# A planned graph network stack: picks and messages in fewer engines, and a planner that counts PE's results as late

## The chip, the cores and the metric

The kernel runs on one NeuronCore of a Trainium2 chip. The metric is the device time of one execution in microseconds (us). The engines are named as in the profile: PE (TensorE, matmuls; PEld its weight loads), DVE (VectorE), ACT (ScalarE), POOL (GpSimd) and SP (SyncE, which here only issues DMAs).

## The reference

Four layers of a graph network over 4096 nodes of 128 features, with one adjacency matrix `adj` of 4096x4096, float32, in which about one entry in a thousand is set, more in the first rows and columns. Every layer adds its result to `x`:

```python
# before each layer
h = jnp.maximum(_layernorm(x, axis=-1), 0.0)
# layer 0
x = x + h @ W_self.T + (adj @ h) @ W_neigh.T + b
# layer 1: Chebyshev terms T0 = h, T1 = adj @ h, T2 = 2 * adj @ T1 - T0
x = x + T0 @ w[0] + T1 @ w[1] + T2 @ w[2] + bias
# layer 2: attention
H = h @ weight.T
C = alpha_src[None, :] + alpha_dst[:, None]
Tau = adj.T * jnp.exp(jnp.maximum(0.2 * C, C))
att = Tau / jnp.sum(Tau, axis=1, keepdims=True)
x = x + adj.T * att @ H
# layer 3: messages
messages = gelu(s[:, None, :] + d[None, :, :] + msg_b)        # s, d = h @ msg_w halves
aggregated = jnp.einsum('ijd,ij->id', messages, adj)
f = gelu(concat([h, aggregated]) @ upd_w.T + upd_b) + h
x = x + layernorm(f) * ln_w + ln_b
```

## The kernel before, in words

**Sparse work from a dense matrix.** The nodes are sorted so that full rows come first. The kernel reads `adj` once (`read_adj`, `mark`, `scan`), makes flags of it, and from these, on the chip, three kinds of lists: for stripes of 256 rows and of 256 columns the lists of nodes that they touch (`pairs`), and for every block of 128 rows the list of its entries (`entries`). A list is cut in chunks of 128 places, one for each partition. All through the kernel, rows are fetched by such lists with indirect DMAs that POOL issues, one for each chunk (line 553 for all of them): 68 chunks of row lists, 74 of column lists and 158 of entries.

**Stages.** First the scan, with the first product of layer 0 (`Layer.multiply`, line 1138 for the near blocks, 1155 for the fetched rows). Then the products of the layers 0 to 2, while `entries` makes the entry lists and `values` fetches their values into `e_val`. Then `Attention`, by column stripes (1228 to 1254), with `finish_3` behind each stripe. Then `Messages`, by groups of four blocks: `prepare`, `message` for every four chunks of entries, `finish` for the last norm and the store. Where the buffers allow it, stages overlap; the messages of the first block may start under the attention.

**The picks** (in `entries`, lines 882 to 894). For up to four chunks, PE multiplies a selection matrix `sel` with the tables `A` and `B` into a PSUM bank of the kind `picks`: positions in columns 0 to W, differences of codes in W to 2W. ACT copies the positions to SBUF (`ehit`, 887), and DVE does one scalar_tensor_tensor for each chunk (890), which compares with the place's own number, multiplies with the differences and sums up into `packed`.

**A message** (`message`, 1391). For up to four chunks it needs: a selection `sel` (622, 624), the matrices `r` with the edge values (1400), the fetched rows `m` of `d_tab` (553), then in a PSUM bank of the kind `banks` the sum of `m` (a product with the identity, 1406) and of the block's own rows picked by `sel` (1408), then the gelu by ACT out of the bank (1412), and the product with `r` into the accumulator of the group (1418).

**The last norm** (`finish`, 1425). DVE makes the mean (1445, 1446), ACT the squares (1450) and the root (1453), DVE the reciprocal and mean times reciprocal (1455, 1456), ACT the scaled copies, one for each block (1459), DVE the weights and sums (1463 to 1465), SP the store (1467).

**The order.** Every piece of work is a task, a generator that yields what it wants next: an engine with an estimate of its time, a free buffer of a kind (`Slots`), or an event. `Plan.run` (299) simulates all tasks in the time of these estimates and at each step lets the one go on that can begin first, or, among those within 0.3 us of it on the same engine, the one with the lowest rank. What it picks is emitted there and then, and `in_order` (348) binds every engine to that order. A step that changes its engine begins `HOP` = 0.2 us after the one before at the earliest (315). Where the plan leaves PE idle for more than 0.8 us, `fill` (604) puts products with zeros into a bank or a pick that is free (609), one for each 0.22 us of 80% of the gap. The kinds that matter here: three `banks`, two `picks`, three `accs`; for messages four tiles `m`, two `r` and one lane with `sel` under the attention, and twelve, four and four afterwards, when the free `picks` join the `banks`. The ranks of the gathers: products and attention 0, columns' segments 4, values of entries 6, the first block's messages 7.

Of the kernel before, what the change touches and what calls it, by code (L numbers as in the profile page):

```python
# [19 lines left out]
AF = mybir.ActivationFunctionType  # L20
ALU = mybir.AluOpType
AX = mybir.AxisListType
# [4 lines left out]
D = 128  # L27
P = 128
# [3 lines left out]
GB = BANK // D  # L32
# [222 lines left out]
class Plan:  # L255
# [4 lines left out]


    HOP = 0.2
    LANDING = 4.0
    BYTES = 330e3
    TABLE = 1.3
# [33 lines left out]
    def run(self, until=lambda: False):  # L299
        while self.tasks and not until():  # L300
            able = []
            for task in list(self.tasks):
                while isinstance(task.want, Event) and task.want.time is not None:
                    if task.want.time + self.HOP > task.ready:
                        task.ready, task.engine = max(task.ready, task.want.time), None
                    self._next(task)
                want = task.want
                if want is None or isinstance(want, Event):
                    continue
                if isinstance(want, Slots):  # L310
                    if not want.free:
                        continue
                    begin = max(task.ready, min(want.free)[0])
                else:
                    begin = max(task.ready + self.HOP * (task.engine != want[0]), self.free[want[0]])
                able.append((begin, task.rank, task.serial, task))
            assert able, [(t.generator.__name__, t.want) for t in self.tasks]
            first = min(able)
            want = first[3].want
            if not isinstance(want, Slots):  # L320

                first = min((a[1:] for a in able if a[0] <= first[0] + min(self.PATIENCE, want[1]) and
                             not isinstance(a[3].want, Slots) and a[3].want[0] == want[0]))
                first = next(a for a in able if a[3] is first[2])
            begin, task = first[0], first[3]
            want = task.want
            if isinstance(want, Slots):
                first = min(want.free)
                want.free.remove(first)
                task.ready = begin  # L330
                self._next(task, want.items[first[1]])
                continue
            duration = want[1]
            if want[0] == "PE":
                duration *= self.PE_TIME
                gap = begin - self.free["PE"]
                if self.filler and gap > self.SHORT:
                    self.filler(self.free["PE"], gap * self.FILLED)
            self.finish = begin + duration
            if len(want) > 2 and want[2] != self.table:  # L340
                self.table = want[2]
                self.finish += self.TABLE
            self.free[want[0]] = self.finish
            task.ready, task.engine = self.finish, want[0]
            self._next(task)
# [12 lines left out]
def on_dve(n):  # L358
    return "DVE", 0.16 + 1.05e-3 * n
# [7 lines left out]
def on_act(n, table=None):  # L367
    return ("ACT", 0.22 + 0.83e-3 * n) + ((table,) if table else ())
# [10 lines left out]
def sparse_stack(tc, x, adj, adjT, diag, w_self, w_neigh, b0, w1, b1, w2, att_src, att_dst,  # L379
# [7 lines left out]
    nc = tc.nc  # L387
    plan = Plan()
    EARLY = 7
    with ExitStack() as ctx:  # L390
# [212 lines left out]

        def fill(begin, time):

            idle = min((free, i, slots.items) for slots in (banks, picks) for free, i in slots.free + [(1e9, 0)])
            if idle[0] < begin - 1.0:
                for _ in range(int(time / 0.22)):
                    nc.tensor.matmul(idle[2][idle[1]], nothing[:, :P], nothing, start=True, stop=True)  # L609

        def rows_of(p, n=GB):
            return p[:, :n * D].rearrange("p (k d) -> p k d", d=D)
# [192 lines left out]
        def entries(number, group):  # L805
# [65 lines left out]
            for i, u in enumerate(units):  # L871
                for g in range(-(-u.cap // GB)):
                    n = min(GB, u.cap - g * GB)
                    yield from selection(lane, mids[:, u.number, :], half[:, u.number:u.number + 1], g, n)
                    for q0 in range(0, n, per):
                        m = min(per, n - q0)
                        k = g * GB + q0
                        p = yield picks
                        pv = p[:, :m * (2 * W + 1)].rearrange("p (q w) -> p q w", w=2 * W + 1)
                        yield "PE", m * (0.3 + 1.3e-3 * W)  # L880
                        for q in range(m):
                            sel = lane["sel"][:, q0 + q, :]
                            nc.tensor.matmul(pv[:, q, :], sel, A[:, i, :], start=True, stop=False)  # L883
                            nc.tensor.matmul(pv[:, q, W:2 * W], sel, B[:, i, :], start=False, stop=True)
                        yield on_act(m * W)
                        hit = lane["ehit"][:, :m * W].rearrange("p (q w) -> p q w", w=W)
                        nc.scalar.copy(hit, pv[:, :, :W])  # L887
                        yield "DVE", m * (0.2 + 1.05e-3 * W) + 0.15
                        for q in range(m):
                            nc.vector.scalar_tensor_tensor(  # L890
                                hit[:, q, :], hit[:, q, :], pos0[:, k + q:k + q + 1], pv[:, q, W:2 * W],
                                op0=ALU.is_le, op1=ALU.mult, accum_out=packed[:, u.chunk + k + q:u.chunk + k + q + 1])
                        nc.vector.tensor_copy(e_row[:, u.chunk + k:u.chunk + k + m], pv[:, :, 2 * W])
                        plan.release(picks, p)
            lo, hi = units[0].chunk, units[-1].chunk + units[-1].cap
# [420 lines left out]
        class Messages:  # L1316
# [74 lines left out]
            def message(self, g, b, u, c, chunks, m, here):  # L1391
                n = len(chunks)
                yield u_done[u.number]
                lane = yield m_lanes
                yield from selection(lane, mids[:, u.number, :], half[:, u.number:u.number + 1], c, n)
                yield self.s_here[g]
                r = yield r_tiles
                yield "DVE", 0.35 * n
                for q, k in enumerate(chunks):
                    nc.vector.tensor_scalar(r[:, q, :], iota_row[:, :P], e_row[:, k:k + 1], e_val[:, k:k + 1],  # L1400
                                            op0=ALU.is_equal, op1=ALU.mult)
                for q in range(n):
                    yield here[q]
                p = yield banks
                yield "PE", n * 0.84
                nc.tensor.matmul(p[:, :n * D], ident, m[:, :n, :], start=True, stop=False)  # L1406
                for q in range(n):
                    nc.tensor.matmul(p[:, q * D:(q + 1) * D], lane["sel"][:, q, :], self.s_rows[g][:, b % GB, :],  # L1408
                                     start=False, stop=q == n - 1)
                plan.release(m_lanes, lane)  # L1410
                yield on_act(n * D, "gelu")
                nc.scalar.activation(m[:, :n, :], rows_of(p, n), AF.Gelu)
                plan.release(banks, p)
                yield "PE", 0.42 * n
                acc = self.acc[g]
                for q in range(n):
                    self.left[b] -= 1
                    nc.tensor.matmul(acc[:, b % GB * P:(b % GB + 1) * P], m[:, q, :], r[:, q, :], start=False,  # L1418
                                     stop=all(self.left[g * GB + k] == 0 for k in range(GB)))
                plan.release(r_tiles, r)  # L1420
                plan.release(messages, m)
                if all(self.left[g * GB + k] == 0 for k in range(GB)):
                    plan.start(self.finish(g), -2)

            def finish(self, g):
# [27 lines left out]
                nc.scalar.activation(st[:, 1, :GB], st[:, 1, :GB], AF.Sqrt, bias=eps, scale=1.0 / D)  # L1453
                yield "DVE", 0.35
                nc.vector.reciprocal(st[:, 2, :GB], st[:, 1, :GB])
                nc.vector.tensor_mul(st[:, 3, :GB], st[:, 0, :GB], st[:, 2, :GB])
                yield "ACT", 0.45 * GB
                for k in range(GB):
                    nc.scalar.activation(f[:, k, :], f[:, k, :], AF.Identity, scale=st[:, 2, k:k + 1],
                                         bias=st[:, 3, k:k + 1])  # L1460
                plan.release(stats, st)
                yield "DVE", 2.1
                nc.vector.tensor_mul(f, f, by_block(ln_w_sb, GB))
                nc.vector.tensor_add(f, f, by_block(ln_b_sb, GB))
                nc.vector.tensor_add(f, f, xN[:, blocks, :])
# [521 lines left out]
```

## Time and profile before

| | us |
|---|---|
| three runs | 1508.06, 1502.92, 1518.15 |
| median | 1508.06 |
| the profiled execution: its own time | 1500.43 |
| its span, from the first to the last instruction | 1498.6 |

| engine | busy us | share of the span | instructions |
|---|---|---|---|
| PE | 1058.5 | 71% | 5943 |
| DVE | 791.5 | 53% | 2982 |
| ACT | 670.3 | 45% | 1344 |
| POOL | 767.3 | 51% | 832 |

The mean granted PE clock is 0.834 of full speed. 216 us of PE's busy time are the products with zeros of line 609. Busy shares are means over stages with different limits. In a line of the waits stand the waiting engine, tile and line, what ended the wait, the sum in us, the number and the longest; in a line of the timeline start, duration, engine, line, operation, tiles and shapes, and in brackets the idle time of the engine ahead of it with what ended it. "issue" means that the profile shows no reason, "remote" and "another core or an unknown queue" that a semaphore came from where the profile can't tell. A group of instructions in the timeline is merged into one line, with x and the number.

### The profile page before, as it was taken

How to read it: one execution, taken by the hardware profiler on the slowest of the kernel's cores; microseconds unless marked ns; L12 is line 12 of the kernel's file. 1: busy time of each engine (PE TensorE's matmuls, PEld its weight loads, DVE VectorE, ACT ScalarE, POOL GpSimd, SP SyncE). 2: the span in 40 equal slices, each digit the busy share in tenths (PEclk: the TensorE clock that was granted, in tenths of full speed). 3: DMA queues.
4: the chain of work that ended last, by engine and by line, in shares of the span. 5: the costliest groups of instructions: out<-in, count | busy, mean ns of one | idle time of the engine just before them, and what ended most of it. 6: DMA issues, size and time to landing. Idle time of an engine off the chain costs nothing.

```text
span 1498.6 us, 19187 instructions
## 1 busy us (share of the span) xinstructions
PE 1058.5 (71%) x5943; PEld 723.0 (48%) x5943; DVE 791.5 (53%) x2982; ACT 670.3 (45%) x1344; POOL 767.3 (51%) x832
## 2 busy tenths in 40 slices
PE   6786788887477867467774289668777955668880
PEld 3454555554256556355653255334444633556660
DVE  5796666886366566355663156334343612344453
ACT  5983666663121212114452087546564801236462
POOL 4135754544455656635667527726576165654500
PEclk9897898888697888677897599879897986888885
DMA  8999999994366778666542045313333121121200
GB/s 252 352 338 318 335 308 342 341 310 145 92 194 191 205 217 232 171 193 176 156 132 80 22 123 146 108 39 87 107 101 97 41 59 43 47 51 48 67 17 17
DMA packets 175415, 236.03 MB, mean 157 GB/s; under 512 B 22452, under 2 KB 155336, under 8 KB 167112
## 3 DMA queue, kind: packets, MB, share of 16 engines
q1 hardware_dynamic: 148904, 186.45, 37.6%
q0 software_dynamic: 26400, 48.27, 13.1%
q8 instruction: 49, 0.80, 0.2%
q14 instruction: 62, 0.51, 0.1%
HBM read 203.41 MB, written 31.23 MB: 157 GB/s over the span
## 4 chain that ended last, share of the span: by engine, by line
PE 26%; issue 11%; ACT 9%; another core or an unknown queue 8%; DVE 5%; DMA 1%; SPq 0%; ACTq 0%; DVEq 0%
PE acc L1254 4%; PE acc L1252 4%; PE bank L597 3%; PE acc L1138 3%; PE acc L1155 2%; PE acc L1418 2%; PE pick L609 1%; PE bank L1406 1%; PE bank L1408 1%; ACT e L1228 1%; ACT junk L1450 1%; ACT e L1231 1%; ACT junk L568 1%; PE pick L1418 1%
## 5 line engine op out<-in xcount | busy, mean ns | idle before, releaser
L553 POOL DMA_INDIRECT e_val<-in_adj,e_at x158 | 155.5, 984 | 48.0 <-issue 46.5
L553 POOL DMA_INDIRECT g<-h_tab,fetch_row x136 | 135.7, 998 | 73.1 <-issue 34.3
L609 PE MATMUL pick<-nothing 128*128 128x512 f16 x532 | 141.4, 413 | 2.4 <-issue 2.4
L1138 PE MATMUL acc<-big,hA 128*128 128x256 f32 x448 | 124.6, 422 | 16.3 <-DMA big<-in_adjT 7.3
L609 PEld LDWEIGHTS <-nothing 128*128 128x128 f16 x795 | 83.5, 108 | 102.7 <-issue 38.3
L553 POOL DMA_INDIRECT g<-a_tab,fetch_col x74 | 77.7, 1049 | 92.5 <-issue 43.6
L553 POOL DMA_INDIRECT rseg<-in_adjT,seg_row x68 | 71.3, 1048 | 94.3 <-issue 39.7
L1138 PEld LDWEIGHTS acc<-big,hA 128*128 128x128 f32 x448 | 90.6, 213 | 32.8 <-DMA big<-in_adjT 8.8
L553 POOL DMA_INDIRECT cseg<-in_adj,seg_col x74 | 70.8, 957 | 66.2 <-DVE pcum L634 23.5
L553 POOL DMA_INDIRECT g<-u_tab,fetch_row x68 | 64.7, 951 | 63.7 <-PE acc L1155 32.5
L890 DVE SCALAR_TENSOR_TENSOR ehit<-ehit,pos,pick 128x32 f32<-128x32 f32 (+7 forms) x158 | 38.8, 285 | 108.0 <-issue 64.6
L1235 DVE TENSOR_TENSOR tau<-e,big 128x512 f32<-128x512 f32 (+3 forms) x61 | 54.2, 889 | 70.2 <-ACT e L1231 43.7
L887 ACT COPY ehit<-pick 128x192 f32<-128x192 f32 (+7 forms) x74 | 20.4, 286 | 157.8 <-remote 72.5
L553 POOL DMA_INDIRECT tau<-d_tab,e_col x63 | 60.5, 961 | 56.2 <-PE acc L1418 15.1
L553 POOL DMA_INDIRECT m<-d_tab,e_col x70 | 68.0, 972 | 38.0 <-issue 16.5
L768 ACT ACTIVATE mask<-dst 128x2048 fp8e4<-128x2048 f32 x43 | 81.8, 1903 | 12.1 <-DMA dst<-in_adj 9.5
L1155 PE MATMUL acc<-big,g 128*128 128x256 f32 x272 | 80.8, 437 | 2.7 <-DMA big<-r_tab 1.9
L622 ACT ACTIVATE sel_t<-iota_row,mids 128x512 f32<-128x512 f32 (+3 forms) x43 | 27.1, 642 | 118.1 <-DVE mids L617 69.8
L568 ACT ACTIVATE junk<-xN,stat 128x128 f32<-128x128 f32 x128 | 51.4, 401 | 60.7 <-DVE stat L564 23.1
L609 PE MATMUL bank<-nothing 128*128 128x512 f16 x263 | 74.8, 430 | 1.6 <-DVE s L1369 1.2
L883 PE MATMUL pick<-eA,esel 128*128 128x65 f16 (+7 forms) x158 | 27.3, 249 | 61.4 <-DVE esel L624 24.1
L1138 PE MATMUL acc<-big,hB 128*128 128x256 f32 x224 | 64.2, 428 | 0.0
(328 smaller groups left out, 2727.5 us busy)
## 6 DMA issues: line engine op xcount, KB each, us to landing
dst<-in_adj SPq DMA_DIRECT2D x43, 1024.0 KB
big<-in_adjT SPq DMA_DIRECT2D x45, 512.0 KB
raw<-in_adj SPq DMA_DIRECT2D x21, 1024.0 KB
big<-in_adjT SPq DMA_DIRECT2D x66, 256.0 KB
big<-r_tab SPq DMA_DIRECT2D x30, 512.0 KB
c_tab<-cseg SPq DMA_DIRECT2D x74, 128.0 KB
r_tab<-rseg SPq DMA_DIRECT2D x68, 128.0 KB
big<-c_tab SPq DMA_DIRECT2D x15, 512.0 KB
```

The lines of the kernel that those rows point to most:

```text
L553: nc.gpsimd.indirect_dma_start(out=dst, out_offset=None, in_=table[:, :], in_offset=bass.IndirectOffsetOnAxis(ap=index, axis=0))
L568: nc.scalar.activation(junk, src[:, k, :], AF.Square, bias=st[:, 0, k:k + 1], accum_out=st[:, 1, k:k + 1])
L597: nc.tensor.matmul(p[:, k * D:(k + 1) * D], lhs[:, k * P:(k + 1) * P], w, start=i == 0, stop=i == len(terms) - 1)
L609: nc.tensor.matmul(idle[2][idle[1]], nothing[:, :P], nothing, start=True, stop=True)
L768: nc.scalar.activation(mask[:, h * HALF:(h + 1) * HALF], raw_of[b, h], AF.Sigmoid, scale=1e38, accum_out=marks[:, 2 * b + h:2 * b + h + 1] ...
L890: nc.vector.scalar_tensor_tensor(hit[:, q, :], hit[:, q, :], pos0[:, k + q:k + q + 1], pv[:, q, W:2 * W], op0=ALU.is_le, op1=ALU.mult, acc ...
L1138: nc.tensor.matmul(acc, self.near[:, b, :D], as_rows(t)[:, k, :], start=count == 0, stop=count == every - 1)
L1155: nc.tensor.matmul(acc, row[:, :D], r, start=count == 0, stop=count == every - 1)
L1235: nc.vector.tensor_mul(tau[:, :n, :], e[:, :n, :], a[:, :n, :])
L1252: nc.tensor.matmul(acc[0:1, CS:2 * CS], parts[k][:, D + 1:], tau[:, k, :], start=False, stop=False)
L1254: nc.tensor.matmul(acc[:, :CS], parts[k][:, :D], e[:, k, :], start=False, stop=self.count[s.index] == every - 1)
L1418: nc.tensor.matmul(acc[:, b % GB * P:(b % GB + 1) * P], m[:, q, :], r[:, q, :], start=False, stop=all(self.left[g * GB + k] == 0 for k in ...
```

## The change

- The planner gets a second constant, `LATE` = 1.5: a step on another engine that follows a step on PE in the same task begins 1.5 us behind it, not 0.2, in the plan. All other handovers keep 0.2.
- `fill` compares free buffers by time and number alone.
- The picks: ACT's copy goes. DVE compares out of PSUM for all chunks of the group at once, multiplies with the differences out of PSUM, and sums up with a tensor_reduce.
- The messages: PE takes a bank and does the selection's product alone, without waiting for the fetched rows, and gives the lane back; then the rows are waited for, DVE adds the bank to them in SBUF and gives the bank back, and ACT does the gelu in SBUF.
- The last norm: mean and reciprocal are applied by DVE, one tensor_scalar for each block; the small product of both goes.

```diff
     HOP = 0.2
+    LATE = 1.5
...
-                    begin = max(task.ready + self.HOP * (task.engine != want[0]), self.free[want[0]])
+                    hop = self.LATE if task.engine == "PE" else self.HOP
+                    begin = max(task.ready + hop * (task.engine != want[0]), self.free[want[0]])
...
-            idle = min((free, i, slots.items) for slots in (banks, picks) for free, i in slots.free + [(1e9, 0)])
+            idle = min(((free, i, slots.items) for slots in (banks, picks) for free, i in slots.free + [(1e9, 0)]),
+                       key=lambda slot: slot[:2])
...
-                        yield on_act(m * W)
+                        yield "DVE", 0.6 + 3.2e-3 * m * W
                         hit = lane["ehit"][:, :m * W].rearrange("p (q w) -> p q w", w=W)
-                        nc.scalar.copy(hit, pv[:, :, :W])
-                        yield "DVE", m * (0.2 + 1.05e-3 * W) + 0.15
-                        for q in range(m):
-                            nc.vector.scalar_tensor_tensor(
-                                hit[:, q, :], hit[:, q, :], pos0[:, k + q:k + q + 1], pv[:, q, W:2 * W],
-                                op0=ALU.is_le, op1=ALU.mult, accum_out=packed[:, u.chunk + k + q:u.chunk + k + q + 1])
+                        nc.vector.tensor_tensor(hit, pv[:, :, :W], pos0[:, k:k + m, None].to_broadcast([P, m, W]),
+                                                op=ALU.is_le)
+                        nc.vector.tensor_mul(hit, hit, pv[:, :, W:2 * W])
+                        nc.vector.tensor_reduce(packed[:, u.chunk + k:u.chunk + k + m], hit, axis=AX.X, op=ALU.add)
                         nc.vector.tensor_copy(e_row[:, u.chunk + k:u.chunk + k + m], pv[:, :, 2 * W])
...
+                p = yield banks
+                yield "PE", n * 0.42
+                for q in range(n):
+                    nc.tensor.matmul(p[:, q * D:(q + 1) * D], lane["sel"][:, q, :], self.s_rows[g][:, b % GB, :],
+                                     start=True, stop=True)
+                plan.release(m_lanes, lane)
                 for q in range(n):
                     yield here[q]
-                p = yield banks
-                yield "PE", n * 0.84
-                nc.tensor.matmul(p[:, :n * D], ident, m[:, :n, :], start=True, stop=False)
-                for q in range(n):
-                    nc.tensor.matmul(p[:, q * D:(q + 1) * D], lane["sel"][:, q, :], self.s_rows[g][:, b % GB, :],
-                                     start=False, stop=q == n - 1)
-                plan.release(m_lanes, lane)
+                yield on_dve(n * D)
+                nc.vector.tensor_add(m[:, :n, :], m[:, :n, :], rows_of(p, n))
+                plan.release(banks, p)
                 yield on_act(n * D, "gelu")
-                nc.scalar.activation(m[:, :n, :], rows_of(p, n), AF.Gelu)
-                plan.release(banks, p)
+                nc.scalar.activation(m[:, :n, :], m[:, :n, :], AF.Gelu)
...
-                nc.vector.tensor_mul(st[:, 3, :GB], st[:, 0, :GB], st[:, 2, :GB])
-                yield "ACT", 0.45 * GB
                 for k in range(GB):
-                    nc.scalar.activation(f[:, k, :], f[:, k, :], AF.Identity, scale=st[:, 2, k:k + 1],
-                                         bias=st[:, 3, k:k + 1])
+                    nc.vector.tensor_scalar(f[:, k, :], f[:, k, :], st[:, 0, k:k + 1], st[:, 2, k:k + 1], op0=ALU.add,
+                                            op1=ALU.mult)
                 plan.release(stats, st)
-                yield "DVE", 2.1
+                yield "DVE", 3.3
```

## The prediction

> **What bounds the kernel now.** I read the page first (shares, chain), then the waits, the chain stage by stage, and the timeline where the chain shows holes. The page ends its span with a chain in which no engine dominates:
>
> ```profile
> span 1498.6 us, 19187 instructions
> PE 26%; issue 11%; ACT 9%; another core or an unknown queue 8%; DVE 5%; DMA 1%; SPq 0%; ACTq 0%; DVEq 0%
> ```
>
> PE holds 26%, but 19% is "issue" or "another core or an unknown queue": nobody worked. (The chain is followed back only to about 595 us.) The list of waits says who stands idle for reasons that the profile can't name:
>
> ```profile
> ACT ehit L887 <- remote: 72.5, 7, 29.2
> PE bank L597 <- issue: 72.5, 13, 44.3
> DVE ehit L890 <- issue: 64.6, 20, 26.9
> ACT tau L1412 <- remote: 61.4, 3, 35.2
> POOL e_val L553 <- issue: 46.5, 153, 0.3
> ```
>
> This is one core, so "remote" can't be another one. L887 and L1412 are the ScalarE instructions that read a PE result in the picks and in the messages: exactly the two hops that go. The timeline shows what they wait for; columns are start, duration, instruction, idle time before it:
>
> ```profile
> 1211.43 1.05 PE L1408 MATMUL bank<-s,msel 128*128 128x128 f32 x8
> 1216.56 0.60 ACT L1412 ACTIVATE tau<-bank 128x512 f32<-128x512 f32 x1 [15.36 <-remote]
> ...
> 1217.21 1.17 PE L1418 MATMUL pick<-r,tau 128*128 128x128 f32 x8 [4.08 <-ACT tau L1412]
> ...
> 1224.29 0.41 DVE L1380 TENSOR_SCALAR r<-ident,diag_sb 128x128 f32<-128x128 f32 x1 [6.00 <-remote]
> ...
> 1229.19 0.50 DVE L1380 TENSOR_SCALAR r<-ident,diag_sb 128x128 f32<-128x128 f32 x1 [4.50 <-remote]
> ...
> 1234.78 0.29 DVE L1380 TENSOR_SCALAR r<-ident,diag_sb 128x128 f32<-128x128 f32 x1 [5.09 <-remote]
> ...
> 1253.00 0.60 ACT L1412 ACTIVATE tau<-bank 128x512 f32<-128x512 f32 x1 [35.24 <-remote]
> ```
>
> The four products of L1418 were through at 1218.4; VectorE, which rewrites the four parts of `r` that they read, is let on at 1224.3, 1229.2, 1234.8 and 1240.4, one part each five microseconds. The gelu at 1253.0 reads a bank that PE had filled at 1221.8. All that time POOL issues one gather each 1.25 us, and at 1253, behind the end of that burst (1247.1), everything comes at once. Such a burst also stands from 806 to 851, where the other engines do nearly nothing:
>
> ```profile
> 820.00:825.00 5.00, 0.00 (x0) 0.00 (x0) 0.00 (x0) 0.00 (x0) 3.78 (x5) 0.50 0.20 51
> ```
>
> (busy PE, PE loads, DVE, ACT, POOL, PE clock, DMA.) So in this kernel **PE's results reach their readers late while POOL gathers back to back**: at once in quiet stretches (a product ends at 1440.47, its gelu starts at 1440.51), about 5 us each in a burst, in order, so that they queue up. The bound is this latency in stages two to four, not an engine. In the first 350 us DMA is 0.91 busy and bounds.
>
> **What the Trainium skill says.** "Perfetto Trace Analysis", Tensor Engine Instruction: the end shown for a matmul is an estimate, and the spread of its semaphore isn't in the profile. The trace agrees: 31 us between end and reader at 1253. "SBUF — State Buffer", two separate sides: a VectorE operation in a two-port mode and GpSimd lock each other out of a shared port, while PE and ScalarE have their own. That isn't the delay here, since ScalarE waits in the longest hole. "TensorE: Matmul & The Clock Gate", Part 1: an idle PE falls to half clock. The trace agrees (0.50 in the line above). No page gives a price for late results under gathers; the price is the trace's.
>
> **The change, stage by stage.** Against the profiled execution's 1500.4 us (span 1498.6; the median shown is 1508.1). Bounds of the stages, from busy times by window: scan to 350, layers to 806, attention to 1195, messages to 1424 (POOL's last gather), tail.
>
> *Picks* (stage two; 69 of 74 instructions of L887 lie there). Away go 74 ACT copies (20.4 us busy) and 158 scalar_tensor_tensor with their accumulator reads (39.3 us by the line's busy time). In come three operations for each of 74 groups. Their twin exists in the row lists (L659, L661, L662: compare out of PSUM, multiply, reduce): 128x128 takes 286, 294, 286 ns, 128x32 takes 181, 191, 185, thus about 0.15 us + 1.05 ns an element. L890's shapes (50x32, 26x104, 22x56, 18x48, 16x40, 12x136, 7x192, 7x200) hold 11,416 elements, 154 to a group: 0.31 us each, 0.35 with the wait for the one before (the twins start 0.33 apart at 128). 74 x 3 x 0.35 = 78 us: VectorE gains 39 us of 456 (257 busy before). It isn't full; "DVE ehit" is 1.4% of the stage's chain, 6.4 us, so doubling costs +7. The ACT copy in the chain gives back 0.3 us and a handover in perhaps ten places: -3. More important: ScalarE no longer stands in front of late picks (157.8 us of idle time before L887), with the layers' evacuations queued behind; VectorE still does (108.0 before L890, part of it inherited from ACT).
>
> *Messages* (stage four). 98 identity products (L1406) go: 46.2 us of PE, 41.4 behind 1195, 6.8% of the stage's chain of 229 us = -15.6. 49 additions come on VectorE: 20,224 elements (158 chunks of 128) at 1.05 ns + 49 x 0.16 = 29 us; L1369, the same form, shows 0.69 at 512. VectorE was 34% busy there; where L1406 stood on the chain, some 17 times, an addition now does: 17 x 0.69 = +12. The gelu reads SBUF: 0.63 (L1376) for 0.60, +1. The order turns: the selection's product runs before the gather lands, so a late PE result overlaps the gather, and gather to gelu passes VectorE only. "Another core or an unknown queue" is 23.8% of this chain, 54.5 us, mostly gelus waiting. Lower bound 0 (the queue of late results moves to `r`, `m` and bank releases, which still need PE); upper bound all. I take 40%: -22.
>
> The bank is now taken before the gather has landed. Under attention two `r` tiles allow two such messages, which may hold two of three banks for over 100 us (the first `r` is made at 1000, its gather starts at 1131). The finishing chains take their banks one after another anyway: +3, at worst +15.
>
> *Norm.* 8 x 4 scaled copies (13.1 us ACT) become 8 x 4 tensor_scalar (L1400's form starts every 0.26 us). A finish goes from 1405.9 to 1409.15 to about 1.1 us: -2.0 for each of the last two, -4; earlier ones are covered.
>
> *Order.* LATE adds 1.3 us to each handover PE to ACT or DVE within a task. Readers move back in their queues and ready work moves up; no work is added but fillers. Those stand in 103 bursts (795 products, 0.22 us apart); 1.3 x 0.8 / 0.22 makes up to four more in each planned gap. At worst 100 x 0.9 us on a PE that is on the chain for a quarter: +20; at best a warmer clock (0.82 to 0.85 in these stages): -10. I take 0. Results that come on time or five late are both badly met by 1.5: of the holes (issue and unknown: 14.7% of 456 = 67 us; 34.4% of 389 less the 44-us burst = 90; 12.8% of 229 = 29) I take an eighth, a tenth and a fifth: -8, -9, -6. Bounds: +25 (a burst put in a worse place) and -60.
>
> Sum: layers +7 -3 -8 = -4; attention +3 -9 = -6; messages -15.6 +12 +1 -22 -6 = -31; tail -4. Together -45: 1455 for such an execution; half of the 7.6 us between it and the median added, **1458**.
>
> **Rivals.** (1) *Both big holes go too* (the bursts at 806 and 1202 are split by the new order): -45 more, 1412. For it: they rest on how many gathers stand ready together; against: POOL's ranks are unchanged. (2) *The wait only moves*: late results are limited by count, one in 5 us, and the same PE results are needed for `r`, `m` and accumulators; then the -22, the holes' -23 fall away and 1500 remains. For it: L1380's four waits are releases, not readers. (3) *Slower: VectorE becomes the one that waits.* It is the busiest of the two, and in order. Now 74 picks and 49 additions put late PE results, and landings, straight on it; behind them stand the layers' sums, the selections and `r`. Price: 108.0 us of idle time over 74 groups was 1.5 us each; 49 more at 1.5 = 73, plus 39 + 29 more work, 141 us of VectorE; at a third on the chain +47, less the sure -16 -4: about 1527, and 1545 with the fillers' worst. It decides once VectorE's idle time before compare and addition exceeds 200 us.
>
> **Numbers.** Forecast 0.43 (own range 1430 to 1490), rival 1 0.14, rival 2 0.15, rival 3 0.28. 1% is about what a measurement here can tell from no change. Faster 0.57, same 0.15, slower 0.28. Range 1405 to 1545: into both outer cases.
>
> **What would show it.** Right: ACT's waits on "remote" at the gelu fall under 20 us; messages to last gather under 200 us; PE busy falls by some 40 us less new fillers; DVE busy rises by about 75. Wrong: a long hole before the new compare or addition on DVE; filler products over 1200; attention over 410 us with PE waiting for banks; the bursts as long as before with the same holes.

## The result, and the profile after

The kernel after is slower, a little: 1516.8 us (median of 20 runs, 1495.5 to 1534.0) against 1502.1 for the kernel before, ratio 1.014 [1.010, 1.017]. The ratio takes only the runs of each kernel that lie within 1.5% of its fastest, so it isn't the quotient of the two medians, which is 1.010. The profiled execution took 1505.1 us (span 1503.2); it was forecast at 1455 and the median at 1458. The two profiled executions differ by 4.6 us only, so the stages below account for a part of the loss.

```profile
span 1503.2 us, 19132 instructions
PE 1049.6 (70%) x5976; PEld 714.1 (48%) x5976; DVE 852.4 (57%) x2961; ACT 644.2 (43%) x1240; POOL 759.9 (51%) x832
PE 39%; DVE 21%; another core or an unknown queue 15%; issue 10%; ACT 8%; DMA 4%; POOL 1%; SPq 1%; DVEq 0%; ACTq 0%; POOLq 0%
```

The work moved as meant: DVE +61 us (791.5 before), ACT -26, PE -9 (46 us of identity products gone, 131 fillers more, which are 32 us). In the chain "another core or an unknown queue" and "issue" still hold much: from 600 us on, which both chains cover, 31.6% before and 29.0% after. To see where the time went, I cut both spans at five events: the last mask of the scan, the attention's first instruction on ScalarE (L1229 after, L1228 before), its last product, POOL's last gather, the end. (The prediction cut the layers at 806, where the value burst began; the attention's start is the steadier mark.) Columns: window, length, busy PE, PE loads, DVE, ACT, POOL with instructions, PE clock, DMA share, GB/s. Before:

```profile
0.00:339.00 339.00, 266.55 (x1975) 171.12 (x1976) 250.86 (x750) 225.08 (x367) 162.12 (x212) 0.87 0.92 321
339.00:864.00 525.00, 336.33 (x1756) 257.92 (x1754) 273.53 (x1511) 130.50 (x317) 295.81 (x313) 0.80 0.55 158
864.00:1183.00 319.00, 257.17 (x1101) 142.49 (x1102) 146.21 (x320) 196.21 (x407) 171.79 (x167) 0.89 0.34 97
1183.00:1424.00 241.00, 166.53 (x930) 126.42 (x928) 87.89 (x258) 82.87 (x173) 137.41 (x143) 0.83 0.21 51
1424.00:1498.00 74.00, 31.93 (x185) 25.06 (x185) 32.96 (x146) 35.60 (x82) 0.18 (x1) 0.70 0.06 17
```

and after:

```profile
0.00:341.00 341.00, 256.50 (x1957) 166.92 (x1958) 250.14 (x742) 224.89 (x367) 158.26 (x210) 0.88 0.92 319
341.00:895.00 554.00, 357.96 (x1845) 262.90 (x1843) 285.10 (x1353) 110.59 (x242) 321.98 (x338) 0.82 0.51 148
895.00:1204.00 309.00, 270.28 (x1193) 151.88 (x1194) 168.61 (x409) 202.51 (x414) 147.28 (x147) 0.90 0.37 104
1204.00:1430.00 226.00, 131.10 (x770) 105.31 (x768) 108.90 (x295) 78.02 (x157) 132.34 (x137) 0.79 0.20 53
1430.00:1503.00 73.00, 33.72 (x217) 27.13 (x217) 39.63 (x166) 28.24 (x63) 0.00 (x0) 0.76 0.06 17
```

The attention gives 10 us, the messages 15, the tail 1; the layers lose 29, the scan 2. Look at POOL's count in the second window: 338 instructions instead of 313, and 110 of them are value gathers (`e_val`), which stand low in rank, instead of 82. Twenty-eight more of these are issued before the attention begins; at 1.25 us each that is 35 us of POOL. Counted in POOL's order, 118 of the 158 come ahead of the attention's first own gather (before: 89), and 56 ahead of the last gather of the third layer (before: 37). The last burst in front of the attention grew from 45 gathers (794 to 850) to 56 (814 to 883). Its first value gather comes at 816 instead of 797, so 17 of the 29 us lie ahead of it (with the scan's 2 taken off) and 12 behind. The standstill stayed, PE's part of it 31 us long instead of 44:

```profile
835.00:860.00 25.00, 0.00 (x0) 0.00 (x0) 3.19 (x19) 0.17 (x1) 18.90 (x21) 0.52 0.02 1
```

The list of waits shows who stands still now (six of its lines). No gelu waits on "remote" any more; other readers of PE, or those waiting for its releases, do, and the gelu (L1415) waits for VectorE's addition (L1412):

```profile
ACT junk L570 <- DVE stat L566: 89.3, 11, 44.2
ACT agg L1165 <- remote: 70.1, 7, 16.2
DVE ehit L890 <- remote: 48.8, 5, 18.3
ACT tau L1415 <- DVE tau L1412: 37.7, 7, 25.2
DVE r L1401 <- remote: 36.0, 8, 23.0
DVE xN L1028 <- remote: 35.7, 3, 26.8
```

The hole that was a late gelu before is now VectorE waiting to write `r`. The trace doesn't name what it waits for; PE's products alone read `r`, so it is most likely their release. VectorE's addition and then the gelu stand behind it:

```profile
1248.67 0.35 DVE L1401 TENSOR_SCALAR r<-iota_row,e_row,e_val 128x128 f32<-128x128 f32 x1 [2.36 <-remote]
...
1272.46 0.34 DVE L1401 TENSOR_SCALAR r<-iota_row,e_row,e_val 128x128 f32<-128x128 f32 x1 [22.98 <-remote]
...
1275.49 0.68 DVE L1412 TENSOR_TENSOR tau<-tau,bank 128x512 f32<-128x512 f32 x1
1276.21 0.63 ACT L1415 ACTIVATE tau<-tau 128x512 f32<-128x512 f32 x1 [25.16 <-DVE tau L1412]
```

The experiments need one more fact. The kernels ran in sessions; the kernels of one session share its runs of the kernel before. In three sessions PE's results came late under gathers, as in both profiles above, and the kernel before took 1502 to 1549 us. In the trace before, 229 of 1021 increments of PE's semaphore come more than 1 us behind the end of the latest product ahead of them, and 252 of 1024 in the trace after. (Some increments are missing in these traces: the kernel before has 1179 products that make one.) In the other three sessions they came on time (3 of 1177 over 1 us in e12 below, all at the very end), and it took 1195 to 1196 us. POOL gathers at the same pace in both. I call them **late** and **prompt** sessions; ratios are within a session. Their intervals are too: the kernel after has 1.014 [1.010, 1.017] here and 1.002 [0.999, 1.006] in the second late session (e5), so two sessions differ by 1% where nothing was changed.

### The profile page after: what moved, and what is told of

Read it like the earlier page. It is cut to its first block, busy times and chain, and to the rows that moved or that the text cites. A ratio compares the mean times of both kernels' runs of the same rounds, so it can differ in the third digit from the quotient of the medians.

```text
span 1503.2 us, 19132 instructions
## 1 busy us (share of the span) xinstructions
PE 1049.6 (70%) x5976; PEld 714.1 (48%) x5976; DVE 852.4 (57%) x2961; ACT 644.2 (43%) x1240; POOL 759.9 (51%) x832
## 4 chain that ended last, share of the span: by engine, by line
PE 39%; DVE 21%; another core or an unknown queue 15%; issue 10%; ACT 8%; DMA 4%; POOL 1%; SPq 1%; DVEq 0%; ACTq 0%; POOLq 0%
PE acc L1139 6%; PE acc L1255 5%; PE acc L1156 5%; PE acc L1253 5%; PE bank L599 3%; PE pick L612 3%; PE bank L612 2%; PE acc L1420 2%; DVE cand L800 2%; DVE col_raw L786 1%; PE bank L1406 1%; ACT junk L570 1%; DVE words L791 1%; DVE words L793 1%
## 5 line engine op out<-in xcount | busy, mean ns | idle before, releaser
L612 PE MATMUL pick<-nothing 128*128 128x512 f16 x583 | 154.9, 415 | 3.3 <-issue 3.1
L612 PEld LDWEIGHTS <-nothing 128*128 128x128 f16 x926 | 97.5, 107 | 119.9 <-issue 41.4
L555 POOL DMA_INDIRECT g<-a_tab,fetch_col x74 | 74.0, 1000 | 85.2 <-PE acc L1255 25.1
L612 PE MATMUL bank<-nothing 128*128 128x512 f16 x343 | 93.0, 417 | 3.8 <-DVE f L1440 1.9
L890 DVE TENSOR_TENSOR ehit<-pick,pos 128x208 f32<-128x208 f32 (+8 forms) x74 | 23.2, 313 | 98.8 <-remote 48.8
L1401 DVE TENSOR_SCALAR r<-iota_row,e_row,e_val 128x128 f32<-128x128 f32 x158 | 46.7, 350 | 57.3 <-remote 36.0
L555 POOL DMA_INDIRECT e<-d_tab,e_col x50 | 48.3, 966 | 44.7 <-DVE msel L627 23.6
```

The source lines that it names most:

```text
L555: nc.gpsimd.indirect_dma_start(out=dst, out_offset=None, in_=table[:, :], in_offset=bass.IndirectOffsetOnAxis(ap=index, axis=0))
```

## The experiments

All had five timed rounds. Stage lengths are of the one profiled execution, cut as above; "layers" is the second window.

**Prompt session (kernel before 1195.2 us).** The change was taken apart: e1 the order alone, e2 the edits without it, e3 and e4 halves of the edits.

```diff
# e1: before, with fill() as changed, and
+    LATE = 1.5
+                    hop = self.LATE if task.engine == "PE" else self.HOP
# e2: after, and
-                    hop = self.LATE if task.engine == "PE" else self.HOP
+                    hop = self.HOP
# e3: before, with fill() as changed and the hunks of entries() (picks)
# e4: before, with fill() as changed and the hunks of message() and finish() (messages, norm)
```

> The kernel before with only the planner's LATE of 1.5 us and the fillers' key; picks, messages and norm as before. Theory A (the new order is what costs: it shifts decoding and value gathers into one longer burst, so stage two ends later): ratio to before 1.015 to 1.03, stage two (first attention L1228's counterpart) starting at 880 to 900 instead of 864. Theory B (VectorE carries the picks and waits for late PE results): ratio 0.99 to 1.00, attention starting at 855 to 870. Theory C (any change of estimates deals the order anew; results scatter without adding up): anything within 0.985 to 1.02, not matched by the sum with the other parts.

> The kernel after with its picks, messages and norm, but planned with 0.2 us for every handover, as before. Theory A: ratio 0.98 to 0.99 (the parts gain what was forecast in the messages and the order took it away). Theory B: ratio 1.01 to 1.02, as the kernel after, with DVE's idle time before the new compare above 90 us. Theory C: within 0.985 to 1.02, and e1 x e2 differs from the kernel after's 1.0138 by over 0.01.

> The kernel before with only the new picks (compare, multiply, reduce on VectorE out of PSUM), planned with 0.2 us. Theory A: 0.99 to 1.00, attention starts at 855 to 866. Theory B: 1.015 to 1.03, attention starts at 880 to 900, DVE's waits before the compare above 90 us. Theory C: scatter, attention starts anywhere from 850 to 900, following the length of the value gathers' longest burst (45 gathers before) at 1.25 us each.

> The kernel before with only the new messages (sum on VectorE, bank taken before the gather) and the new norm, planned with 0.2 us. Stage two is untouched by the edit. Theory A: 0.975 to 0.985, as forecast for messages (-31) and tail (-4); messages from attention's end to the last gather below 210 us. Theory B: 0.985 to 1.00, messages 215 to 225 us since additions wait for PE as the gelus did. Theory C: scatter of the messages stage, set by the burst behind attention (36 gathers in both kernels).

Measured: e1 1.032 [1.028, 1.035], e2 1.008 [1.005, 1.012], e3 1.013 [1.010, 1.016], e4 1.007 [1.005, 1.010]. Attention begins at 716, 680, 692 and 677. Theory A is right in sign on e1 and wrong on e2: the edits gain nothing here. (Its ranges and starts were meant for late results.) In e4 the messages take 199 us against 196 before (e12), although PE has 23 us less to do:

```profile
945.00:1144.00 199.00, 141.74 (x903) 118.34 (x902) 132.36 (x362) 96.24 (x194) 140.87 (x143) 0.86 0.24 63
```

POOL's 143 instructions at 1.25 us are 179 of these 199 us: with results on time POOL's gathers come near to filling this stage, so the gelu's path is hardly its limit. Theory B is right in sign on e3 (layers 380 us instead of 373 in e12), but its tail is longer too (64 instead of 49), which that edit doesn't touch; and e2, which has the same picks, has layers of 370 us. And e3 and e4 don't add up to e2 (1.013 x 1.007 = 1.020, not 1.008): something other than the edits' own cost is in these numbers.

**Late session (before 1536.9 us).** The whole change, a meaningless shift of the planner, and e1 and e2 again.

```diff
# e5: after
# e6: before, and
-    HOP = 0.2
+    HOP = 0.3
# e7: e1 again
# e8: e2 again
```

> The kernel after, whole. In e1 to e4 the chip gave every PE result on time (1185 of 1188 increments of PE's semaphore within 0.05 us) and the kernel before took 1195 us. Theory D (the order made for late results costs 3% where results are on time, and gains about as much where they are late): ratio 1.03 to 1.045 if results are on time here (e1 x e2 = 1.040), 1.014 if they are late. Theory C (scatter): on time, anywhere in 1.00 to 1.03.

> The kernel before with the planner's handover of 0.3 us instead of 0.2, for all engines alike: no instruction added, no idea in it, only the order dealt anew. Theory C: a ratio off 1 by 0.005 or more, either way. Theory D: within 0.995 to 1.005, since 0.1 us is nothing; then differences of 0.7 to 1.3% between parts are the parts' own.

> The kernel of e1 (order alone) once more, for a chip on which PE's results come late under gathers. Theory D: 0.97 to 0.99 if they are late here, 1.03 if on time. Theory A (the new order costs in any case): 1.02 to 1.03 on both.

> The kernel of e2 (picks, messages and norm, planned as before) once more, for a chip on which PE's results come late. Theory D: 1.02 to 1.04 if late (the parts put late results on VectorE and the order takes half of it back), 1.008 if on time. Theory A: 0.98 to 0.99 if late.

Measured: e5 1.002 [0.999, 1.006], e6 1.020 [1.014, 1.027], e7 1.016 [1.009, 1.023], e8 0.996 [0.993, 1.000]. Three things follow. A shift with no idea in it costs 2%, as much as any part of the change: single orders scatter by that much, and a difference of 1% between two orders says little on the idea behind one of them. The edits do help in the messages where results are late: these take 229 us in e8 and 224 in e5, but 247 in e6 and e7, which have the old ones (e7, then e8):

```profile
1216.00:1463.00 247.00, 171.36 (x946) 128.54 (x944) 88.49 (x256) 83.41 (x173) 133.98 (x140) 0.84 0.19 50
```

```profile
1222.00:1451.00 229.00, 133.83 (x808) 107.47 (x808) 111.51 (x302) 80.89 (x165) 138.05 (x141) 0.79 0.20 53
```

And e5 against e8, which differ in LATE alone and share the session, show where the order loses: in the layers, 572 us instead of 553 (e5, then e8), with 338 of POOL's instructions instead of 311:

```profile
359.00:931.00 572.00, 374.91 (x1850) 277.17 (x1849) 287.64 (x1357) 111.36 (x244) 322.49 (x338) 0.79 0.49 145
360.00:913.00 553.00, 365.40 (x1792) 271.73 (x1789) 297.36 (x1405) 115.53 (x251) 297.82 (x311) 0.79 0.52 152
```

The price that theory D put on the edits, 1.02 to 1.04, is not there, nor its gain from the order alone. The whole change is 1.006 of e8 here; in the prompt sessions it is 1.020 of e2 (1.028 of e13 by 1.008, from two sessions).

**Prompt session (before 1196.5 us).** Pacing, LATE in half of the plan, a second meaningless shift, and the kernel before for its profile.

```diff
# e9: before, with fill() as changed, in values()
-                        yield GATHER
+                        yield "POOL", 2.4
                         gather(e_val[:n, k:k + 1], adj_flat, e_at[:n, k:k + 1])
+                        for _ in range(4):
+                            nc.gpsimd.memset(pace, 0.0)
# e10: after, and
-    LATE = 1.5
+    LATE = 0.2
+        plan.LATE = 1.5
         last = Messages()
# e11: before, and
-    HOP = 0.2
+    HOP = 0.25
# e12: before
```

> The kernel before, with four memsets of an unused tile (128x256, about 0.3 us each) on POOL behind each of the 158 value gathers, planned at 2.4 us a piece: the gathers of a burst come every 2.4 us instead of 1.25. Nothing else is changed. Where PE's results come late, theory E (gathers back to back make them late, not the number of gathers): the stretch of 45 gathers in which the other engines stand still goes, fewer than 180 of about 1020 increments of PE's semaphore over 1 us late (229 before), ratio 0.96 to 0.985. Theory F (each gather costs its share of lateness however it is spaced, or POOL's busy time does): ratio 1.00 to 1.04, since POOL gets 175 us more. Where results come on time: 1.00 to 1.05, POOL being the busiest engine behind PE and VectorE there.

> The kernel after, but LATE is 0.2 us in the plan of the scan and of the layers and 1.5 us only from the attention on. Theory G (LATE in the layers' plan clumps the value gathers into one burst of 56 to 61 instead of 44 to 46, and this is where the change loses): longest burst 44 to 46 again, attention starting where it does with the parts alone (680 with results on time, 913 on the late chip), ratio 0.975 to 0.995 late, 1.00 to 1.015 on time. Theory C (any new deal of the order): no prediction of sign; 0.99 to 1.03.

> The kernel before with the planner's handover at 0.25 us instead of 0.2: a second meaningless shift. Theory C (any new deal is worse than the one that was kept, by 1 to 3%): 1.005 to 1.03. Theory G: 0.99 to 1.01 unless its longest burst differs from 45 by more than 5 gathers, 1.25 us for each.

> The kernel before, run as a kernel of its own for its profile on this chip: ratio 0.995 to 1.005. With results on time, all theories: attention starts at 670 to 685, and no increment of PE's semaphore is over 1 us late but the last few; late: as in the first profile, 864 to 915.

Measured: e9 1.172 [1.169, 1.176], e10 1.009 [1.006, 1.013], e11 1.017 [1.014, 1.020], e12 1.002 [0.999, 1.004]. e9 is a miss: results came on time, so it says nothing on theories E and F, and its 200 us of memsets stand on POOL ahead of the messages' gathers, so that the messages wait for the values:

```profile
DVE e_val L949 <- DMA e_val<-in_adj,e_at: 206.7, 26, 29.2
ACT L1416 <- PE pick L1412: 182.1, 1, 182.1
```

e10 has LATE where the attention and messages are planned and costs no more than e2; its layers take 374 us. e11 repeats e6's lesson with results on time: layers 380, tail 60 instead of 49. Its shift has no idea in it, but it too puts more value gathers ahead of the attention's first gather (99, before 89).

**Prompt session (before 1196.5 us).** The whole change, the mirror of e10, and other deals of both.

```diff
# e13: after
# e14: after, and
+        plan.LATE = 0.2
         last = Messages()
# e15: after, and
-    LATE = 1.5
+    LATE = 1.3
# e16: e2, and
-    HOP = 0.2
+    HOP = 0.25
```

> The kernel after once more, for a chip with results on time, where it has not been timed. If on time: theory G (LATE in the layers' plan costs about 30 us of stage two, the parts bring nothing where results are on time) gives 1.03 to 1.045, attention starting at 705 to 720 against 687 before; theory C gives no number, 1.00 to 1.04. If late: 1.00 to 1.02 as in the two measurements there are.

> The mirror of e10: the kernel after with LATE 1.5 us in the plan of scan and layers, and 0.2 us from the attention on. Theory G: as the kernel after or slower; on time 1.025 to 1.045 with attention starting at 705 to 720; late 1.005 to 1.03 with a longest burst of 55 to 61 gathers. Theory C: not tied to the half that has LATE; as often below e10's 1.009.

> The kernel after with LATE 1.3 us instead of 1.5: the same idea, another deal. Theory G: within 0.01 of the kernel after on this chip, attention starting 15 us or more later than with 0.2 us. Theory C: differs from the kernel after by 0.01 or more.

> The kernel of e2 (parts, planned without LATE) with a handover of 0.25 us: another deal of the parts. Theory C: on time 1.00 to 1.03, off e2's 1.008 by 0.005 or more; late 0.98 to 1.02. If the parts have a gain of their own under late results, it stays below the 1.02 that the meaningless shift of the kernel before (e6) gave.

Measured: e13 1.028 [1.025, 1.031], e14 1.036 [1.033, 1.038], e15 1.020 [1.017, 1.023], e16 1.009 [1.006, 1.013]. Theory G holds in its main point: LATE costs where the scan and the layers are planned (e14), not behind them (e10). Two of its numbers are missed: e13 lies a little under 1.03, and in e15 the attention starts at 697, 9 to 17 us behind the kernels with the edits and 0.2 or 0.25 us there (680 to 688), not 15 or more. Theory C wanted e16 off e2 by 0.005, and it isn't. With LATE in the layers' plan the four prompt ratios are 1.020, 1.028, 1.032 and 1.036; with 0.2 to 0.25 us there they are 1.002 to 1.017, seven kernels (e9 with its memsets left out). The groups don't overlap, though e11 (1.017) and e15 (1.020) lie within each other's intervals. The layers' windows of e12 (before), e16 (edits, no LATE), e15 (1.3) and e13 (1.5):

```profile
314.00:687.00 373.00, 311.25 (x1722) 239.59 (x1720) 272.72 (x1510) 130.21 (x316) 263.65 (x275) 0.90 0.76 221
```

```profile
312.00:687.00 375.00, 310.03 (x1766) 232.61 (x1764) 296.14 (x1404) 115.19 (x250) 269.06 (x282) 0.94 0.75 223
```

```profile
308.00:697.00 389.00, 330.16 (x1834) 250.30 (x1833) 288.17 (x1364) 114.77 (x249) 279.10 (x292) 0.91 0.72 214
```

```profile
314.00:709.00 395.00, 334.69 (x1852) 250.49 (x1850) 286.64 (x1356) 111.69 (x244) 283.01 (x295) 0.91 0.70 209
```

Length and POOL's count rise together: 373, 375, 389, 395 us with 275, 282, 292, 295 instructions; 20 more at 1.25 us are 25 us, and the stage is 22 us longer. The picture on POOL at the attention's first gather, e12 and then e13:

```profile
742.66 0.94 POOL L553 DMA_INDIRECT e_val<-in_adj,e_at  x1 [0.30 <-DMA e_val<-in_adj,e_at]
743.91 1.71 POOL L553 DMA_INDIRECT g<-a_tab,fetch_col  x1 [0.30 <-issue]
```

```profile
777.18 0.95 POOL L555 DMA_INDIRECT e_val<-in_adj,e_at  x1 [0.30 <-issue]
778.44 0.95 POOL L555 DMA_INDIRECT g<-a_tab,fetch_col  x1 [0.30 <-issue]
```

It comes straight behind a value gather in both, 34.5 us later in e13; 29 more value gathers ahead of it (118 and 89) make 36. In e2 it comes at 741.4 behind 95, in e15 at 766 behind 113, in e1 at 783 behind 121. Over the eleven prompt kernels other than e9 it is the same: 89 to 99 value gathers ahead go with layers of 369 to 380 us, 113 with 389, 118 with 395, 121 with 404. The counts alone don't say which is cause: a stage that is planned longer also leaves room for more gathers.

**Late session (before 1548.6 us).** Which of the two is the cause was asked by holding value gathers back on POOL, nothing else.

```diff
# e17: after, in values(), and in gathers() behind the last layer
+                        made[0] += 1
+                        if made[0] > 37:
+                            yield listed
+                        if made[0] > 89:
+                            yield a_table
                         yield GATHER
+            listed.set(plan.finish)
# e18: e2, and the same with 30 and 70
```

> The kernel after with LATE of 1.5 us throughout, but its value gathers held back on POOL: the 38th and later ones stand behind the last gather of the third layer, the 90th and later ones behind the attention's table, as they do in the kernel before (37 and 89; in the kernel after 56 and 118). Theory H (LATE loses because the plan, with the layers stretched, finds POOL idle and puts 19 and 29 more value gathers ahead of the layers' and the attention's own gathers, at 1.25 us each): where results are on time the attention starts at 680 to 695 and the ratio is 1.005 to 1.015 instead of 1.028; where late, 0.985 to 1.00. Rival (LATE loses by the order on PE, ACT and VectorE, picks behind layers): attention from 705, ratio 1.02 to 1.035 on time, 1.00 to 1.015 late.

> The kernel of e2 (picks, messages and norm, planned without LATE) with the value gathers held back further: 30 ahead of the layers' last gather (41 in e2) and 70 ahead of the attention's table (95). Theory H: each gather less ahead of the attention is worth up to 1.25 us until the attention's POOL is full (186 of 240 us busy there before): ratio 0.985 to 1.00 on time instead of 1.008, 0.97 to 0.995 late. Rival: no gain, 1.00 to 1.02 on time, and over 1.02 if values come too late for the messages.

Measured: e17 0.987 [0.982, 0.991] on record, e18 1.006 [1.001, 1.010]. The ratio of e17 doesn't stand firm. Its six runs took 1526 to 1544 us, the 27 runs of the kernel before 1523 to 1564. The medians of all runs give 0.989, and against the eight fastest runs of the kernel before it is 0.997. So e17 is no slower than before; that it is faster isn't shown. All three values lie in theory H's range and under the rival's, but the profile doesn't show H's way. In e17 37 value gathers come ahead of the layers' last gather and 99 ahead of the attention's first one, instead of 56 and 118; yet the layers take 557 us (572 in e5, 554 in the first profile of after), the last burst is still 56 gathers long, and the attention takes 320 us (306 and 309):

```profile
344.00:901.00 557.00, 365.42 (x1850) 264.88 (x1849) 285.98 (x1355) 111.31 (x244) 304.20 (x319) 0.81 0.50 149
```

Nineteen of POOL's instructions went out of this stage, and it is no shorter than in the first profile of after. In e18 theory H's 0.97 to 0.995 is missed: with 79 ahead (95 in e8) the layers take 544 us instead of 553, but the attention 324 instead of 309 and the messages 240 instead of 229. The gathers held back come due there.

```profile
358.00:902.00 544.00, 353.59 (x1781) 266.19 (x1782) 294.87 (x1402) 116.28 (x254) 285.42 (x298) 0.79 0.53 154
902.00:1226.00 324.00, 254.64 (x1110) 143.43 (x1110) 152.04 (x341) 193.03 (x396) 187.54 (x182) 0.86 0.32 92
1226.00:1466.00 240.00, 140.81 (x803) 111.16 (x802) 111.37 (x299) 85.23 (x170) 138.32 (x142) 0.74 0.20 52
```

So in e18 what the layers gave the later stages took. And e17 has had no prompt session, where theory H has its best support.

## Why the prediction was wrong

**What failed: the order's term.** LATE was to shrink the holes by 8, 9 and 6 us, 23 in all, and to add no work but fillers. The pair that tests this alone with late results is e8 and e5, and there LATE costs 0.6%, some 9 us: the layers are 19 us longer, the attention 3 and the messages 5 shorter. Without the edits it costs 1.6% (e7). Since a shift with no idea in it moves the time by up to 2%, the sign of so small a loss isn't safe; that the 23 us of gain aren't there is. In the first pair of profiles the layers, forecast at -4, are at +29. What I left out is the queue on which no reader of PE stands. I counted PE, ACT and VectorE. A planner that believes the chain of a layer to be 1.3 us longer at each step sees POOL idle more, and fills it with work of low rank, the value gathers: 28 more of them go ahead of the attention. e10, e13, e14 and e15 place the loss in the plan of scan and layers, where results are on time. That it comes about through POOL is supported by the counts and not shown: e17 took 19 of these gathers out of the layers, and the stage didn't shrink. The rival, a worse order on PE, ACT and VectorE, stays open.

**What failed besides: the edits' term.** Without the order's 23 us the forecast for the edits is -22 (+7 -3 +3 -15.6 +12 +1 -22 -4), or 0.986. e8 measures them alone with late results: 0.996, some -6. The mis-sized step is the one of -22 for gelus that no longer wait.

**Messages.** Forecast -31, measured -15 (226 us against 241), and -18 from e6 to e8, both without LATE. The additions took 28.3 us (29 forecast), and PE's busy time in this stage fell by 35. But ScalarE stood idle 103.0 us before the gelus and stands idle 96.0 now: 66.1 of the 103.0 ended with "remote", and 58.2 of the 96.0 end with VectorE's addition. The addition itself hardly waits (8.6 us). It stands in VectorE's queue behind the writes of `r`, and these wait on "remote", most likely for PE, now (36.0 us) as they did before (40.9 us, lines 1380 and 1400). So the sign "remote at the gelu under 20 us" came true in the letter, and the wait only changed its place. In prompt sessions the gain is nil; POOL's gathers nearly fill the stage there.

**Picks.** Right in size: three instructions of 74 take 23.2, 23.3 and 23.2 us, 70 in all where 78 were forecast with their waits. No run isolates what they cost in the layers: e3 has 380 us where before has 373, but e11, without new picks, has 380 too, and e2, with them, 370. VectorE's late picks are still there (98.8 us of idle time before L890, 108.0 before); a gain from ScalarE standing clear of them doesn't show.

**Attention and tail.** -10 for -6; -1 for -4. Cut at the first value gather of the burst (797 and 816), near the prediction's cut, the layers are at +17 and the attention at +2.

**Fillers and clock.** 926 products, under the 1200 that would have meant trouble, and 32 us more of PE; the mean granted clock went from 0.834 to 0.844. From 600 us on the fillers hold 26 us of the chain before and 31 after. So taking 0 was about right, though no run leaves the fillers out.

**The rivals.** Rival 2 (the wait only moves, 1500 us) came nearest: it gave the size and the place in the messages, and not the loss in the layers. Rival 1 is out: of the two bursts that it names one has 36 gathers as before, the other 56 instead of 45. Rival 3 got the sign, but not its mechanism: VectorE's idle time before compare and addition is 107 us, far from the 200 at which it was to decide, and the edits alone (e8) are at 0.996, not slower.

**Readings.** A share of the chain that the profile gives to no engine isn't time in which nobody worked: after, the chain has a hole of 72 us from 820 to 892, and PE works 16 us in it. The sums have slips of 1 or 2 us (half of 7.6 on 1455 makes 1459, 1527 and 20 make 1547); nothing hangs on them.

**The premise.** I took late results for a trait of this kernel under gathers. The gathers are the same in prompt sessions and the results on time; so gathers back to back go with lateness but don't make it by themselves. LATE, made for late results, costs 0.6 to 1.6% where they are late and 2.0 to 3.2% where they are not.

## What to carry to other kernels

When a planner writes the order, shift one of its constants by a little that means nothing before you credit or blame an idea: here 0.05 and 0.1 us moved the time by 1.7 and 2.0%. When you tell it that one chain is slower, count what it then puts into the idle time of the other queues, the low-ranked work above all, because that work is then run in the order written whether there is idle time or not. When a reader moves to another engine, look at what stands ahead of it in that engine's queue: here the gelu's wait went to the addition, which stood behind `r`. And look at a stage's other limits before pricing a wait taken away: with results on time POOL's gathers nearly filled the messages, and the shorter path beside them gained nothing.

## What the runs showed of the hardware that was not expected

The same kernel takes 1195 us in some sessions and 1502 to 1549 in others. The increments that come more than 1 us late are nearly all PE's: in the trace before 229 of PE, 11 of VectorE and 2 of ScalarE. How much of the 300 us and more they make, no run measures; the scan, too, takes 339 to 364 us in late sessions and 308 to 315 in prompt ones. Here is a stretch of 25 us inside a run of 134 gathers (532 to 700 us) in a prompt session (e12), to be set beside the standstill of the kernel after from 835 to 860 above:

```profile
600.00:625.00 25.00, 22.52 (x146) 18.51 (x143) 21.75 (x128) 15.64 (x36) 18.91 (x20) 0.97 0.70 197
```

POOL is busy 18.9 us of 25 in both. PE works 22.5 us here and 0 there. The burst of 43 value gathers in front of the attention, the same in both, shows it too: PE works 49.6 of 56 us in e12 and 8.6 of 53 in the first profile of before. In the standstill VectorE crept too, one instruction behind another each 1.4 us at times (837 to 844 us), so PE's results may not be all that is slow in the worst bursts. What decides between a late and a prompt session no run here shows. The expectations speak of a late chip, but the record has the same chip number for e9 to e12, which were prompt, and for e17 and e18, which were late; whether gathers spaced out would help in a late one was not measured, since e9 fell into a prompt session.
